# The attention block's output projection: seven products of quarters in two accumulation tiles, from the second image on

## The chip, the cores and the metric

The kernel runs on one core of a Trainium2 chip. A core has TensorE (PE, with its weight loads PEld), VectorE (DVE), ScalarE (ACT), GpSimd (POOL) and SyncE (SP), each with its own in-order queue, and 16 DMA engines that SP, ACT and POOL feed. The metric is the device time of one execution in microseconds, the median of several runs.

## The reference

Eight images of 512 channels by 32 x 32 positions pass two attention layers. Cut to what matters:

```python
# layer 0: eight heads, q, k and v quantized to 8 bits (fake_quant)
h = group_norm(xf, gn_w, gn_b)
q, k, v = split(einsum('oc,bct->bot', qkv_w, h) + qkv_b)
w = softmax(einsum('bct,bcs->bts', q * scale, k * scale))
a = einsum('bts,bcs->bct', w, v)
a = einsum('oc,bct->bot', proj_w, a) + proj_b        # the projection in question
x1 = xf + a
# layer 1: one head over all 512 channels
h = group_norm(x1, ...); q, k, v = h @ wq + bq, h @ wk + bk, h @ wv + bv
out = x1 + (softmax(q k^T / sqrt(512)) v) @ wp + bp
```

The projection is, per image, a 512 x 512 matrix times a 512 x 1024 matrix, all in float32; its bias is one number per channel.

## The kernel before, in words

Channels lie on the 128 partitions in four blocks (`cc`); the 1024 positions are cut into two halves (`hf`). A first phase computes q, k and v of all images and stores them in DRAM. The second phase, where the change lies, runs two things interleaved on every engine: the quantized attention of layer 0 (`attention`, L1018), which is one image ahead, and for the image whose attention is done the projection (`project`, L1296), the norm (`norm1`, L1344, through `norm_steps`, L228) and layer 1 (`layer1`, L1655).

Attention goes by units of 128 keys: a score product into the tile pair `st`, an exponential on ScalarE into `pt` (four buffers), a half-precision copy of it into `two` (by ScalarE, or by GpSimd for every fourth unit), the rest `two<-pt,two` by a VectorE subtraction, then the products `av` over the keys and the row sums `sm`. The sums of each pair of heads are inverted and `divide` (L1185, in `finish`, L1157) scales `ao`, the attention's output, two blocks of 512 columns per pair of heads.

Layer 1 computes its large products by a seven-product scheme for 2 x 2 quarters (`seven`, L1393, of Strassen and Winograd's kind): two PSUM tiles `x` and `y` of 128 x 512, each of them 2 x 256 columns of a quarter; a product is four matmuls of 256 columns for each 256 rows of contraction, and after it one of the outputs is taken out by VectorE or ScalarE while the other tile is filled. The sums and differences of quarters that it needs are VectorE work.

`project` is not in that form. For each half and each block of 128 output channels it adds up four matmuls of 512 columns in one PSUM tile. An eviction (`evict`, L1313) then adds the bias and the input x in place, `h<-pj,vec,h`, and SP stores the sum x1 to DRAM in `x1_d`, from where layer 1 loads it again for its output. A statistic per block (`stats`, L1319, BATCH_NORM_STATS2) is postponed as a chore, and in the second half an aggregate makes mean and variance `gmv` of it. `norm_steps` averages these over a group's channels by a tiny product with `gavg` (`gps_b`), computes the variance over the group, a second such product, and the scale.

From the second image on, `project` and the start of the norm stand inside the last output block of the image before (`o_run`, L1540, with `first` and `more`, L1764 to L1773): after its fourth product comes a piece of attention, the two halves of the projection with a piece of attention between them, another piece of attention, and then the block's three remaining products (`o`), with `gps_b` after the first of them. There the projection uses the two score tiles (`score_bank`, L315), and `load_wp` and `load_x2` (L1260, L1266) have the weights and the input loaded through ScalarE's queue ahead of the block. The last image's projection has no attention left beside it.

The order of each engine's instructions is written when the program is built. The class `InOrder` (L72) keeps a planned time for VectorE, ScalarE and TensorE; `do(cost, work)` puts work in at once with a planned cost, `later(name, cost, work, ...)` leaves it as a chore with a due time, `chore()` and `fill` put chores in where the plan has room, and `settle(name)` puts in all that are left of a name. `awaits` moves TensorE's planned time to that of a result. The planned times set only the order; on the chip each engine takes its instructions strictly in that order and waits where an operand is not ready.

Of the kernel before, what the change touches and what calls it, by code (L numbers as in the profile page):

```python
# [18 lines left out]
P = 128  # L19
# [39 lines left out]
def attn_pair_kernel(  # L59
# [166 lines left out]


    def norm_steps(  # L228
        src, dst, wcol, bank, nm, ccs=range(CC), fine=False, put=None, mv=None, apply=None
    ):  # L230

        n, c0 = len(ccs), ccs[0]
        put = put or (lambda hf, cost, work: work())
        if mv is None:
            st, mv = stat_tiles(n, nm)
            for i, cc in enumerate(ccs):
                for hf in range(NH):
                    dve.bn_stats(st[:, i, hf, :], src(cc, hf))  # L240
                aggregate(mv, st, i)
                if fine and i + 1 < n:
                    yield
        yield
        ps = bank(f"gps_{nm}")[:, 0:n]
        mm(ps, lhsT=gavg, rhs=mv[:, :, 0], start=True, stop=True)

        d = small.tile([P, n], F32, tag=f"gd{n}", name=f"gd_{nm}")
        mean = small.tile([P, n], F32, tag=f"gmean{n}", name=f"gmean_{nm}")

        def offsets():
            dve.tensor_sub(d, mv[:, :, 0], ps)
            dve.tensor_copy(mean, ps)
            dve.tensor_mul(d, d, d)
            dve.tensor_add(d, d, mv[:, :, 1])

        dve.do(0.6, offsets)
        yield
        ps2 = bank(f"gps2_{nm}")[:, 0:n]
        mm(ps2, lhsT=gavg, rhs=d, start=True, stop=True)  # L260
        rstd = small.tile([P, n], F32, tag=f"grstd{n}", name=f"grstd_{nm}")
        dve.do(0.15, lambda: dve.tensor_scalar(rstd, ps2, EPS, None, ALU.add))
        nc.gpsimd.tensor_tensor(rstd, rstd, mhalf[:, 0:n], ALU.pow)
        dve.do(
            0.15, lambda: dve.tensor_mul(rstd, rstd, vec[:, wcol + c0 : wcol + c0 + n]), dve.t + 1.4
        )
        if apply is not None:
            off = small.tile([P, n], F32, tag=f"goff{n}", name=f"goff_{nm}")
            dve.scalar_tensor_tensor(off, mean, -1.0, rstd, ALU.mult, ALU.mult)
            for i, cc in enumerate(ccs):  # L270
                apply(cc, rstd[:, i : i + 1], off[:, i : i + 1])
                yield
            return
        for hf in range(NH):
            for i, cc in enumerate(ccs):
                put(hf, 0.5, lambda i=i, cc=cc, hf=hf: dve.tensor_scalar(
                    dst(cc, hf), src(cc, hf), mean[:, i : i + 1], rstd[:, i : i + 1],
                    ALU.subtract, ALU.mult,
                ))
                if fine and i % 2 == 1:  # L280
                    yield
        if not fine:
            yield
# [23 lines left out]
    with ExitStack() as fast:  # L307
# [710 lines left out]
        def attention():  # L1018
# [138 lines left out]
            def finish(b, j, hf, u):  # L1157

                nm = f"{b}_{j}"
                if hf == 0:  # L1160
                    if b:
                        settle("ao")
                    ao[b, j] = aop.tile([P, NH, 512], F32, tag="ao", name=f"ao_{nm}")
                    if b == 0 and j % 2 == 1:
                        rss[b, j] = kept_u[:, 0:2].rearrange("p h k n -> p h (k n)")
                    else:
                        rss[b, j] = l1p.tile([P, NH, 512], F32, tag="rs", name=f"rs_{nm}")
                aot, rs = ao[b, j], rss[b, j]
                act.do(0.6, lambda: act.copy(aot[:, hf, :], avs.pop((b, j, hf))))
                act.do(0.6, lambda: act.copy(rs[:, hf, :], sms.pop((b, j, hf))))  # L1170
                if hf == 0:
                    return
                del rss[b, j]
                n = b * PAIRS + j

                apart = small.tile([P, 2, 16], F32, tag="apart", name=f"apart_{nm}")
                for w in range(2):
                    nc.sync.dma_start(
                        apart[:, w, :],
                        rs[2 * w * QUAD : 2 * (w + 1) * QUAD : QUAD].rearrange(  # L1180
                            "r h (p k) -> r h p k", k=16
                        ),
                    )

                def divide():  # L1185
                    dve.scalar_tensor_tensor(aot, aot, scl[:, 2:3], rs, ALU.mult, ALU.mult)

                def spread():
                    r = rcs[:, n * 16 : (n + 1) * 16]
                    dve.tensor_add(r, apart[:, 0, :], apart[:, 1, :])  # L1190
                    dve.reciprocal(r, r)
                    nc.sync.dma_start(rs_d[n].rearrange("r (p k) -> (r p) k", k=16), r)
                    for i, r in enumerate(HALF):
                        nc.sync.dma_start(
                            rs[r], rs_d[n][2 * i : 2 * i + 2, :].partition_broadcast(CH)
                        )
                    if InOrder.planned:
                        dve.later("ao", elements(1100), divide, dve.t + 7.0, 20.0)
                    else:
                        dealt.append((u + (20 if j < PAIRS - 1 else 13), "ao", divide))  # L1200

                if InOrder.planned:
                    dve.later("ao", 0.4, spread, pe.t + 5.0, 8.0)
                else:
                    dealt.append((u + (12 if j < PAIRS - 1 else 7), "ao", spread))
# [58 lines left out]
                dma(xts[b][:, :, bass.ts(hf, 512)], x_v[b, :, :, bass.ts(hf, 512)])  # L1264

        def load_wp(b, dma):  # L1266
            wps[b] = l2p.tile([P, CC, C], F32, tag="sums", name=f"wp0_{b}")
            dma(wps[b], w_sq[WP0])

        def load_first(u):  # L1270

# [21 lines left out]
            for t, src in zip(wm_tiles(b), wm_d):  # L1293
                act.dma_start(t, src)

        def project(b, bank=bank):  # L1296

            settle("ao")  # L1300
            st, mvs[b] = stat_tiles(CC, f"b{b}")
            wp0 = wps.pop(b)
            for hf in range(NH):
                for oc in range(CC):
# [6 lines left out]
                    xx = xts[b][:, oc, bass.ts(hf, 512)]  # L1311

                    def evict():  # L1313
                        dve.scalar_tensor_tensor(
                            xx, ps, vec[:, V_PB0 + oc : V_PB0 + oc + 1], xx, ALU.add, ALU.add
                        )
                        nc.sync.dma_start(x1_d[b][oc // 2][hf][:, oc % 2, :], xx)

                    def stats(oc=oc, hf=hf, xx=xx):  # L1319
# [24 lines left out]
        def norm1(b, bank=bank):  # L1344
# [14 lines left out]
                    put(hf, elements(512), work)  # L1359

            for n, _ in enumerate(norm_steps(
                at, at, V_GN1W, bank, f"b{b}", put=put, mv=mvs[b]
            )):
                if n == 2:
                    sums[b] = l2p.tile(
                        [P, 3, NH, CC // 2, 256], F32, tag="sums", name=f"sums2_{b}"
                    )
                    for hf in range(NH):
                        h11, h12, h21, h22 = quarters(b, hf)
                        t1, t2, t4 = (sums[b][:, i, hf] for i in range(3))  # L1370
                        for i, args in enumerate((
                            (t1, h12, h11), (t2, h22, t1), (h12, h22, h12), (t4, h21, t2)
                        )):
                            put_sum(hf, i, lambda args=args: tt(*args, ALU.subtract))
                yield
# [14 lines left out]
            dve.later("o", 0.25, spread, pe.t + 4.0, 5.0)  # L1390
            return rs

        def seven(nm, pairs, keep, whole, add, bank=bank):  # L1393

            nonlocal turn
            turn ^= 1  # L1400
            x, y = (bank(f"{nm}_{i}").rearrange("p (t n) -> p t n", t=2) for i in range(2))

            def product(n, ps, start):
                left, right = pairs[n]
                k = left.shape[1]
                for t in range(2):
                    for i in range(k):
                        mm(
                            ps[:, t, :], lhsT=left[:, i, bass.ts(t, P)], rhs=right[:, i, :],
                            start=start and t == 0 and i == 0, stop=(i == k - 1),  # L1410
                            skip_group_check=True,
                        )
# [4 lines left out]
                (5, x, False, whole, None),  # L1417
            )
            for i, (n, ps, start, out, m) in enumerate(work):
                awaits(free[(i + turn) % 2])  # L1420
                product(n, ps, start)
                free[(i + turn) % 2] = out(ps) if m is None else out(m, ps)
                yield i + 1

        free = [0.0, 0.0]
        turn = 0

        def slots(gq):
# [226 lines left out]
        def layer1(b, steps):  # L1655
# [46 lines left out]
            for hf in range(NH):  # L1702
# [59 lines left out]
                if b + 1 < B and last:  # L1762

                    def first():  # L1764
                        nonlocal ahead
                        yield -1
                        yield from project(b + 1, score_bank)
                        yield 2
                        ahead = norm1(b + 1, score_bank)
                        next(ahead)  # L1770

# [8 lines left out]
        def fold():  # L1780
# [36 lines left out]
            for i, (rows, lw, rw) in enumerate(((wa_rows, NQ1, NK1), (wm_rows, NV1, WP1))):  # L1817
# [29 lines left out]
                    load_first(24)  # L1847
                else:
                    dve.tensor_add(dst, tot, vec[:, V_BP : V_BP + CC])
            (m11, m12), (m21, m22), (v1, v2), (v3, v4) = ([t[:, i] for i in range(2)] for t in wm)  # L1850
            for args in (
                (v1, m11, m12, ALU.subtract), (v2, m22, v1, ALU.subtract),
# [452 lines left out]
```

## Time and profile before

| | |
|---|---|
| runs | 2558.69 us median of three (2558.62 to 2561.11) |
| profiled execution | 2559.32 us, its span 2557.2 us |
| granted TensorE clock | 0.999 |
| TensorE busy | 2515.9 us (98%) |
| VectorE busy | 1897.6 us (74%) |
| ScalarE busy | 1346.5 us (53%) |
| GpSimd busy | 186.0 us (7%) |
| DMA | 250.70 MB, mean 98 GB/s |
| pj matmuls (records of 512 columns) | 512, busy 224.1 us |
| evictions h<-pj,vec,h | 64 of 749 ns on average |

A row of groups gives the engine, the operation, what is written from what (buffer numbers left out), the shapes and the count; then the busy time, the mean of one record in nanoseconds, and the idle time of the engine just ahead of such an instruction with what ended it. A float32 matmul leaves two records. In the chain of waits each row is a start, a length and the engine that held up the end; in a timeline, a start, a length and, in brackets, how long the engine had been idle and for whom. Image numbers count from 0; image 2's projection runs from 1171.0 to 1203.5 us.

### The profile page before, as it was taken

To read this page: it belongs to the slowest core of one execution; us is meant where nothing else is said; L and a number is where in the kernel's file an instruction comes from. 1 tells how busy PE (TensorE), PEld (TensorE's weight loads), DVE (VectorE), ACT (ScalarE), POOL (GpSimd) and SP (SyncE) were. 2 spreads that over 40 slices of the span, in tenths; PEclk is the share of its full clock that TensorE was granted. 3 is DMA by queue.
4 is the path that set the end of the run, shared out by engine and by line. 5 is a ranking of instruction groups with operands and counts; after the bars stand their busy time and mean duration, and the time that the engine had idled before them with its cause. 6 is when DMAs were issued, how large, how long until landed. Compare 5 with 4: busy or idle time off the path is not lost.

```text
span 2557.2 us, 38727 instructions
## 1 busy us (share of the span) xinstructions
PE 2515.9 (98%) x15670; PEld 1746.2 (68%) x15670; DVE 1897.6 (74%) x2747; ACT 1346.5 (53%) x1685; POOL 186.0 (7%) x167
## 2 busy tenths in 40 slices
PE   8999999999999999999999999999999999999998
PEld 4788888873357756775777577667756775777787
DVE  7887776668887778777877787777778777885544
ACT  3332223319857655665666466656655665664121
POOL 0000000001100001000100100010101000100000
PEclk9999999999999999999999999999999999999999
DMA  4533333236622232223313222322232123212211
GB/s 168 177 142 125 131 124 122 109 131 162 162 88 63 79 116 85 58 74 122 98 57 100 92 79 78 110 92 63 79 112 88 55 71 128 96 42 80 87 38 39
DMA packets 160717, 250.70 MB, mean 98 GB/s; under 512 B 27152, under 2 KB 93712, under 8 KB 159120
## 3 DMA queue, kind: packets, MB, share of 16 engines
q1 hardware_dynamic: 125792, 182.81, 21.6%
q10 hardware_dynamic: 30560, 57.71, 6.5%
q0 software_dynamic: 4176, 7.60, 1.7%
q8 instruction: 125, 2.05, 0.3%
q14 instruction: 64, 0.52, 0.1%
HBM read 153.64 MB, written 86.28 MB: 94 GB/s over the span
## 4 chain that ended last, share of the span: by engine, by line
PE 85%; DVE 5%; ACT 2%; issue 1%; DMA 1%; POOL 0%; SPq 0%; ACTq 0%; DVEq 0%
PE s L209 15%; PE o L209 13%; PE qkps L209 12%; PE pj L209 8%; PE av L209 8%; PE v2ps L209 7%; PE vps L209 6%; PE g L209 6%; PE st L209 4%; PE sm L209 3%; DVE two L91 2%; ACT pt L91 1%; PE fold L209 1%; DVE h L91 1%; DVE acc L91 0%
## 5 line engine op out<-in xcount | busy, mean ns | idle before, releaser
L91 ACT ACTIVATE pt<-st,esc 128x1024 f32<-128x1024 f32 x467 | 496.4, 1114 | 332.1 <-PE st L209 317.6
L91 DVE TENSOR_TENSOR two<-pt,two 128x1024 f16<-128x1024 f32 x467 | 561.5, 1216 | 131.0 <-POOL two L1092 100.7
L91 ACT CAST two<-pt 128x1024 f16<-128x1024 f32 x346 | 350.8, 1055 | 6.9 <-ACT p L91 5.1
L1092 POOL CAST two<-pt 128x1024 f16<-128x1024 f32 x112 | 146.0, 1304 | 1409.4 <-PE sm L209 746.3
L209 PE MATMUL av<-two,v 128*32 128x512 f16 x3968 | 245.9, 381 | 2.5 <-DVE two L91 2.1
L209 PE MATMUL s<-g,h 128*128 128x256 f32 x1024 | 233.4, 380 | 0.0
L209 PE MATMUL pj<-ao,wp 128*128 128x512 f32 x512 | 224.1, 595 | 0.6 <-DVE h L91 0.6
L209 PEld LDWEIGHTS s<-g,h 128*128 128x128 f32 x1024 | 192.9, 190 | 31.0 <-issue 4.3
L91 ACT ACTIVATE u_ring<-qkps,qkbt 128x512 f32<-128x512 f32 x89 | 60.9, 685 | 243.8 <-PE qkps L209 219.3
L209 PEld LDWEIGHTS <-v 128*32 128x32 f16 x3968 | 91.8, 96 | 140.0 <-issue 66.7
L209 PEld LDWEIGHTS pj<-ao,wp 128*128 128x128 f32 x512 | 96.0, 190 | 122.5 <-issue 110.8
L209 PE MATMUL s<-g,sums 128*128 128x256 f32 x768 | 178.4, 381 | 0.2 <-DVE p L91 0.2
L209 PE MATMUL o<-p,v 128*128 128x256 f32 x768 | 175.2, 382 | 1.0 <-DVE p L91 1.0
L209 PE MATMUL st<-q,k 64*128 64x512 bf16 x1024 | 163.4, 382 | 11.9 <-ACT pt L91 7.5
L209 PEld LDWEIGHTS o<-p,v 128*128 128x128 f32 x768 | 144.3, 190 | 27.1 <-issue 5.7
L209 PEld LDWEIGHTS s<-g,sums 128*128 128x128 f32 x768 | 144.7, 190 | 24.2 <-issue 4.6
L209 PE MATMUL sm<-two,ones 128*32 128x512 f16 x1984 | 136.0, 379 | 0.0
L209 PEld LDWEIGHTS <-k 64*128 64x128 bf16 x1024 | 34.8, 94 | 143.8 <-issue 142.2
L209 PE MATMUL qkps<-half,w_high 128*128 128x512 f32 x480 | 132.4, 398 | 0.0
L209 PE MATMUL qkps<-half,w_mix 128*128 128x512 f32 x480 | 130.6, 394 | 1.0 <-DVE half L91 1.0
L209 PE MATMUL qkps<-half,w_low 128*128 128x512 f32 x480 | 130.5, 394 | 0.0
L209 PE MATMUL v2ps<-wm,h 128*128 128x256 f32 x512 | 119.9, 383 | 1.9 <-ACT g L91 1.3
(226 smaller groups left out, 3902.2 us busy)
## 6 DMA issues: line engine op xcount, KB each, us to landing
rs<-rs_d SPq DMA_DIRECT2D x76, 256.0 KB
x<-in_x_dram SPq DMA_DIRECT2D x32, 512.0 KB
q_d<-wa SPq DMA_DIRECT2D x32, 512.0 KB
k_d<-wa SPq DMA_DIRECT2D x32, 512.0 KB
v_d<-v_ring SPq DMA_DIRECT2D x32, 512.0 KB
raw<-q_d SPq DMA_DIRECT2D x32, 512.0 KB
raw<-k_d SPq DMA_DIRECT2D x32, 512.0 KB
x_d<-h SPq DMA_DIRECT2D x64, 256.0 KB
```

The lines of the kernel that those rows point to most:

```text
L91: ins = self.latest = op(*args, **kw).ins
L209: ins = nc.tensor.matmul(ps, lhsT=lhsT, rhs=rhs, **kw).ins
L1092: copy(two[:, 0], pt)
```

## The change

From the second image on, the projection is done by `seven` as well. The weights' four sums are made once, during image 0's projection (`combine_wp`), and written to DRAM in `wp_d`; later images load three of the quarters from the weights, and the sums from `wp_d`, the last of them into layer 1's tile `vt` by a load of its own in `project_seven`. The sums over the attention's output are made in place in `ao` and in a free part of `vt`. The three outputs of a product form that need two additions get both from VectorE into the tile of x itself: each of the seven products of a half is followed by one VectorE addition `h<-pj,h` of 2 x 256 columns, and the two PSUM tiles are the two score tiles, as before. The stores to `x1_d` go by quarters. The bias is no longer added at the eviction: it is added to the means ahead of `gps_b` and subtracted again from the group mean (`shift`), and added to `ob`, the bias of layer 1's output. Image 0 keeps the old form, without the bias.

```diff
@@ norm_steps
+        if shift is not None:
+            dve.do(0.15, lambda: dve.tensor_add(mv[:, :, 0], mv[:, :, 0], shift))
         ps = bank(f"gps_{nm}")[:, 0:n]
         mm(ps, lhsT=gavg, rhs=mv[:, :, 0], start=True, stop=True)
...
-            dve.tensor_copy(mean, ps)
+            if shift is None:
+                dve.tensor_copy(mean, ps)
+            else:
+                dve.tensor_sub(mean, ps, shift)
@@ finish, divide
                     dve.scalar_tensor_tensor(aot, aot, scl[:, 2:3], rs, ALU.mult, ALU.mult)
+                    if b and j == 1:
+                        first_sums(b)
@@ load_wp
-            wps[b] = l2p.tile([P, CC, C], F32, tag="sums", name=f"wp0_{b}")
-            dma(wps[b], w_sq[WP0])
+            wps[b] = w = l2p.tile([P, 6, CC // 2, C // 2], F32, tag="sums", name=f"wp0_{b}")
+            dma(w[:, 0:2].rearrange("p i k n -> p (i k) n"), w_sq[WP0][:, :, 0 : C // 2])
+            dma(w[:, 2], w_sq[WP0][:, CC // 2 :, C // 2 :])
+            dma(w[:, 3:6], wp_d[:, 0:3])
+        def combine_wp():
...
+            for args in (
+                (s1, a21, a22, ALU.add), (s2, s1, a11, ALU.subtract),
+                (s3, a11, a21, ALU.subtract), (s4, a12, s2, ALU.subtract),
+            ):
+                dve.later("wc", elements(512), lambda args=args: tt(*args), within=20.0)
+            dve.later("wc", 0.0, lambda: nc.sync.dma_start(wp_d, wc[:, 0:4]), within=20.0)
+        def first_sums(b):
+            for cc in range(CC // 2):
+                h = ao[b, cc]
+                dve.later("at", elements(512), lambda h=h: tt(
+                    h[:, :, 256:512], h[:, :, 256:512], h[:, :, 0:256], ALU.subtract
+                ), within=30.0)
+        def project_seven(b, room):
+            settle("at")
+            settle("ao")
+            st, mvs[b] = stat_tiles(CC, f"b{b}")
+            w = wps.pop(b)
+            a11, a12, a22, s2, s3, s1 = (w[:, i] for i in range(6))
+            t2 = room[:, 0 : NT // 2, 0:256].rearrange("p (k h) n -> p k h n", h=NH)
+            s4 = room[:, NT // 2 : NT // 2 + 2, 0:256]
+            act.dma_start(s4, wp_d[:, 3])
+            left, right = slice(0, 256), slice(256, 512)
+            def second(k):
+                tt(t2[:, k], ao[b, 2 + k][:, :, right], ao[b, k][:, :, right], ALU.subtract)
+            for k in range(2):
+                dve.do(elements(512), lambda k=k: second(k))
+            for hf in range(NH):
...
+                def into(q, row, col, full, hf=hf):
+                    def add(ps):
+                        there = dve.do(elements(512), lambda: tt(q, ps, q, ALU.add))
+                        if full is not None:
+                            nc.sync.dma_start(x1_d[b][row][hf][:, :, col * 256 : (col + 1) * 256], q)
+                        return there
+                    return add
...
+                for step in seven(
+                    f"pj_{b}_{hf}",
+                    ((a11, h11), (a12, h21), (s2, th), (s3, h11), (s1, t1), (s4, h22), (a22, h21)),
+                    lambda n, ps: keeps[n](ps), into(q12, 0, 1, 1), lambda n, ps: adds[n](ps),
+                    score_bank, True,
+                ):
+                    if step in (1, 2):
+                        for k in range(2):
+                            h = (h11, h21)[step - 1][k]
+                            args = (h, th[k], h) if step == 1 else (h, h, th[k])
+                            dve.do(elements(256), lambda args=args: tt(*args, ALU.subtract))
+                    for oc in {6: (2, 3), 7: (0, 1)}.get(step, ()):
+                        dve.later("pj", 0.62 + 0.2 * hf, lambda oc=oc, stats=stats: stats(oc), within=4.0)
+                    chore()
+                if hf + 1 < NH:
+                    yield -1
@@ project, image 0
-                        dve.scalar_tensor_tensor(
-                            xx, ps, vec[:, V_PB0 + oc : V_PB0 + oc + 1], xx, ALU.add, ALU.add
-                        )
+                        dve.tensor_tensor(xx, ps, xx, ALU.add)
@@ layer1, first
-                        yield from project(b + 1, score_bank)
+                        yield from project(b + 1, vt)
                         yield 2
+                        settle("pj")
                         ahead = norm1(b + 1, score_bank)
@@ fold
                     dve.tensor_add(dst, tot, vec[:, V_BP : V_BP + CC])
+                    dve.tensor_add(dst, dst, vec[:, V_PB0 : V_PB0 + CC])
```

`norm1` passes the projection's bias as `shift` in every image, and waits for the weight sums (`settle("wc")`) in image 0. `seven` takes a right operand as a list of blocks, and with its new argument `alone` it plans with two free tiles of its own.

## The prediction

> **What bounds the kernel now.** I read the page's parts 1 and 2 first, then the groups of part 5.
>
> ```profile
> PE 2515.9 (98%) x15670; PEld 1746.2 (68%) x15670; DVE 1897.6 (74%) x2747; ACT 1346.5 (53%) x1685; POOL 186.0 (7%) x167
> PEclk9999999999999999999999999999999999999999
> L209 PE MATMUL pj<-ao,wp 128*128 128x512 f32 x512 | 224.1, 595 | 0.6 <-DVE h L91 0.6
> ```
>
> TensorE is busy 98% at full clock, and the projection hardly waits (0.6 us). So TensorE time taken out counts, as long as nothing else becomes late. The price of both forms comes from the chain of waits over the whole span; its five longest pieces hold the last image's projection (no attention beside it), and a block in the seven-product form:
>
> ```profile
> 2362.57 27.47 PE pj L209 x64
> 2412.93 24.17 PE v2ps L209 x112
> ```
>
> Records: a float32 product leaves two. 64 records of 512 columns take 27.47 us (0.429 each), 112 of 256 columns 24.17 us (0.216 each).
>
> Next the chain in the window 1195 to 1225 us, around the end of image 2's projection, and the VectorE timeline over the same stretch:
>
> ```profile
> 1194.95 8.58 PE pj L209 x20
> 1203.54 0.98 PE av L209 x16
> ...
> 1207.45 3.65 PE o L209 x16
> 1211.10 0.12 PE gps_b L209 x2
> ```
> ```profile
> 1204.36 0.69 DVE L91 BATCH_NORM_STATS2 gst_b<-h 128x6 f32<-128x512 f32 x1
> 1205.09 0.21 DVE L91 BATCH_NORM_AGGREGATE gmv_b<-gst_b 128x2 f32<-128x12 f32 x1
> 1207.13 1.23 DVE L91 TENSOR_TENSOR two<-pt,two 128x1024 f16<-128x1024 f32 x1 [1.83 <-POOL two L1092]
> 1211.13 0.69 DVE L91 TENSOR_TENSOR kept_u<-o,kept_u 128x512 f32<-128x512 f32 x1 [2.78 <-PE o L209]
> ```
>
> After the projection TensorE needs 7.5 us to reach gps_b, the product that averages the means over groups. The means were ready at 1205.30, 5.6 us early. That slack is what the change spends. Last, the busy time by stretch (columns: length, PE, PEld, DVE, ACT, POOL):
>
> ```profile
> 1171.00:1185.00 14.00, 14.00 (x38) 6.05 (x35) 11.27 (x16) 4.04 (x6) 0.00 (x0) 1.00 0.55 170
> 1189.50:1203.50 14.00, 14.00 (x40) 6.03 (x40) 8.80 (x13) 3.46 (x4) 0.00 (x0) 1.00 0.24 87
> 1218.50:1240.00 21.50, 21.50 (x176) 14.70 (x172) 21.40 (x31) 15.25 (x21) 4.21 (x2) 1.00 0.34 117
> ```
>
> VectorE is free for 2.7 and 5.2 us in the two projection halves, and for 0.1 us in the stretch that starts 15 us later.
>
> **Part by part.** *The products.* Seven images go from 32 products of 512 columns to 56 of 256: 27.47 - 24.17 = 3.30 us each, 23.1 us in all. A rule speaks against this. The Trainium skill ("TensorE: Matmul & The Clock Gate", Back-to-back issue gap) says that in a stream of weight loads and matmuls the spacing depends on both, about 81 ns at 128 columns and 131 ns at 512, so narrower products are nearly as dear as wide ones. On a straight line between (my estimate from that page) 256 columns cost 98/131 = 0.75 of 512: the image would take 27.47 x 112/64 x 0.75 = 36 us, 8.6 us more than now and 60 us over seven. The rows say 0.216/0.429 = 0.50. They are of this kernel's float32 products, with one 190 ns weight load per record, so I take the row.
>
> *VectorE, per image.* Removed: eight evictions of 750 ns. Added: fourteen of 512 elements from PSUM (row p<-s,kept_u: 689 ns), four 512-element subtractions (687 ns) and eight of 256 elements, which no row shows in this form: 0.35 us (the 256-element tensor-scalar row, 347 ns) to 0.51 us (the x<-kept_u row); I take 0.42, as half of 687 plus the fixed part that the 4-element rows show (0.15). Sum: 14 x 0.69 + 2.75 + 3.4 - 6.0 = 9.8 us. Two of the 512-element ones come much earlier, at the second pair's division, in a stretch where VectorE is busy 16 to 17 of 20 us: cost nothing. The rest, 8.4 us, meets 7.9 us free in the two halves, which also get shorter by 3.3 us. So some of the present work must move, and the instruction order tells which: the four "two" subtractions (1.12 us from start to start in a row) that now stand between the evictions of the second half, and three of its four statistics (0.85 us each with the aggregate), all follow the last eviction; in the first half it is three "two" and three statistics.
>
> *Inside a half* I lay the in-order queues side by side: a product every 1.73 us, its eviction starting 0.29 us after it (as now), one 512-element operation every 0.61 us when queued. In the first half two second sums end before the first eviction; all evictions meet their product, and a tile is reused 0.7 us after it is free. Half one ends with 5.8 us of postponed vector work, done just before the first eviction of half two. No stall inside.
>
> *After the last product*, in VectorE order: wait 0.29, eviction 0.61, four "two" 4.48, three statistics 2.55, one "two" 1.12, the eviction kept_u<-o 0.61, the new addition of the bias to the means 0.20 with its hand-over: 9.86 us until gps_b may start. Now it starts after 7.46. The new wait is 2.4 us, with what is queued behind it on TensorE: two products of the output block and everything that follows. Its bounds: were no work postponed, the addition would still stand behind kept_u<-o, 0.29 + 0.61 + 0.20 = 1.1 us after that product; were everything as above and the "two" slowed by GpSimd's casts, perhaps 3. I take 2.4. Afterwards VectorE is free for some 2 us before the next eviction, so no debt reaches the full stretch.
>
> *ScalarE.* Three loads in place of one are issued at 1148 us, and a cast is queued behind an exponential. The chain there is vector work with no slack (kept_u, acc, p, then TensorE, from 1158.94 on), so up to 0.35 us; exponentials whose buffers wait for the postponed "two": up to 0.25. Below, both are nothing, since ScalarE has 1.55 us free at 1160.8. I take 0.1 in all.
>
> *DMA.* Weights grow from 1.0 to 1.75 MB per image plus 1 MB written once, 6.25 MB on 250.7. The load is issued at 1148 and wanted at 1171; queue 10 moved 57.71 MB in 6.5% of the span, about 350 GB/s while active, so 3.5 MB with the input need some 10 us. The last sum's 256 KB are issued at 1172 and wanted at 1181. The stores of x1 keep number and bytes in half as long rows; SP's fetch of the next v falls behind the first store, to 1175.5, and is wanted at 1195. Nothing, if the loads land within these margins; past them, microsecond for microsecond.
>
> *Image 0 and once.* Four sums for the combined weights: one stands ahead of the first eviction, which TensorE already awaits (0.65 us), so 0.6; three fall into an idle 2.4 us. The bias addition before gps_b, where nothing hides it: 0.2. Together 0.8 lost. *Image 7* has no attention beside it, so nothing is postponed but three statistics: 3.30 - 1.1 = 2.2 gained.
>
> **Sum.** Images 1 to 6: 3.30 - 2.4 - 0.1 = 0.8 each, 4.8; plus 2.2, minus 0.8: 6.2 us. The profiled execution took 2559.32 us (span 2557.2 and 2.1 around it), so 2553.1; it lay 0.6 above the median of the runs, 2558.69, so the median becomes 2552.5.
>
> **Rivals.** *Debt repaid early*: the postponed subtractions run in gaps that I miss, and only the 1.1 us behind kept_u<-o remain. For it: 15.7 us of VectorE idle between 1171 and 1218. Against: the queue is in order. 6 x 2.2 + 2.2 - 0.8 = 14.6, 2544. *All of it*: nothing waits, 23 us, 2535.6; against it stands the addition's place in the queue. *Gain eaten*: wait at gps_b 3 us and ScalarE's 0.6 in full: 6 x (-0.3) + 1.4, no change, 2556 to 2561. *Slower*: VectorE becomes the bound. Its work from the projection's start to gps_b, some 35 us, runs longer than reckoned, as TENSOR_SCALAR does beside GpSimd (0.74 us alone, one of 1.49 at 1168.56); the surplus delays gps_b one for one and, beyond 2 us, enters the full stretch. From 1.0 us per image the gain is gone, from 1.9 it is slower by 0.2%; at 2.5, 2561 to 2570. Against: two-source operations show few long records. *Narrow products dear*, as the rule says: about 2615. *Not doing what it says*: the order holds the seven products for images 1 to 7, so no.
>
> **How the numbers follow.** A measurement here tells some 0.2% (5.1 us) from no change: faster is below 2553.6. Likeliest case, 2549 to 2556, 0.56, of which 0.38 lies below; debt repaid 0.16; all 0.04; eaten 0.15; slower 0.08; rule 0.01. Faster 0.38 + 0.16 + 0.04 = 0.58, same 0.18 + 0.15 = 0.33, slower 0.09. The range reaches from 2544 to 2560; the likeliest case's own is 2549 to 2556.
>
> **What would show it.** Right: pj records 784 for images 1 to 7 at 0.216 us, each half's products within 12.3 us, gps_b waiting for DVE gmv_b by about 2.4 us in images 1 to 6 and 1.1 in image 7, kept_u<-o no longer idle before it. Wrong: waits among the products (evictions late), gps_b on time, PE waiting for a DMA of wp, or losses in the stretch after gps_b.

## The result, and the profile after

The changed kernel takes 2575.23 us (median of four runs, 2573.62 to 2578.86) against 2558.97 us for the kernel before (median of four by then): ratio 1.006, 95% interval 1.0048 to 1.0072. It is 16.3 us slower, where 6.2 us less had been forecast. The profiled execution of it took 2573.62 us, with a span of 2571.8 us, 14.6 more than before; the clock was 0.998.

The lines of the page and the group of the projection's products, after the change:

```profile
PE 2501.7 (97%) x16006; PEld 1811.0 (70%) x16006; DVE 1965.1 (76%) x2886; ACT 1348.8 (52%) x1685; POOL 188.7 (7%) x167
L209 PE MATMUL pj<-ao,wp 128*128 128x256 f32 (+1 forms) x624 | 155.1, 404 | 1.0 <-DVE h L91 1.0
```

The last row holds the products that read ao and wp; with those that read the sums, images 1 to 7 have 784 records, as forecast. TensorE is busy 14 us less: the products give the 23 us (12.30 us a half in the chain below, for 13.95), while the av and st records, which now wait, show 6.5 more. The first half of image 2 in the chain of before:

```profile
1171.09 13.95 PE pj L209 x32
```

VectorE is busy 67 us more, about as reckoned. The span less TensorE's busy time rose from 41.3 to 70.1 us, so the question is where TensorE waits. I cut both spans at two kinds of record on TensorE's timeline, the first pj of an image and its gps_b, and compare the pieces (image 0's row starts at the span's start):

| stretch (us) | before | after | difference | forecast |
|---|---|---|---|---|
| start to gps_b of image 0 | 727.9 | 729.0 | +1.2 | +0.8 |
| six times gps_b to the next image's first pj | 1204.8 | 1216.5 | +11.7 | +0.6 |
| six times first pj to gps_b, images 1 to 6 | 239.5 | 240.1 | +0.6 | -5.4 |
| gps_b of image 6 to first pj of image 7 | 190.2 | 190.3 | +0.1 | 0 |
| image 7, first pj to gps_b | 30.9 | 30.9 | 0.0 | -2.2 |
| gps_b of image 7 to the end | 163.9 | 164.9 | +1.0 | 0 |

Most of the loss, 1.9 us in each of six images, lies where the prediction looked for 0.1: ahead of the projection. Laid side by side, the two TensorE timelines run in step from gps_b for 182 us and part at one block of attention. TensorE's waits there follow from ScalarE's timeline. Before:

```profile
1148.06 0.60 ACT L91 ACTIVATE p<-s 128x512 f32<-128x512 f32 x1 [0.37 <-PE s L209]
1148.06 0.35 ACTq L91 DMA_DIRECT2D wp<-in_w_sq_dram  x1
1148.45 1.00 ACTq L91 DMA_DIRECT2D h<-in_x_dram  x2
1149.50 1.05 ACT L91 CAST two<-pt 128x1024 f16<-128x1024 f32 x1 [0.85 <-ACT p L91]
1151.51 0.58 ACT L91 COPY kept_u<-o 128x512 f32<-128x512 f32 x1 [0.96 <-PE o L209]
```

and after, at the same place:

```profile
1151.26 0.60 ACT L91 ACTIVATE p<-s 128x512 f32<-128x512 f32 x1 [0.37 <-PE s L209]
1151.26 1.59 ACTq L91 DMA_DIRECT2D wp<-in_w_sq_dram  x2
1152.90 0.48 ACTq L91 DMA_DIRECT2D wp<-wp_d  x1
1153.42 1.00 ACTq L91 DMA_DIRECT2D h<-in_x_dram  x2
1154.71 0.58 ACT L91 COPY kept_u<-o 128x512 f32<-128x512 f32 x1 [2.86 <-DMA wp<-in_w_sq_dram]
1155.19 1.12 ACT L91 ACTIVATE pt<-st,esc 128x1024 f32<-128x1024 f32 x1
1156.20 1.04 ACT L91 CAST two<-pt 128x1024 f16<-128x1024 f32 x1
```

ACTq rows are transfers that ScalarE issues; p<-s runs beside the first of them, and no other ScalarE work starts until the last is issued. From the start of p<-s to the cast it took 1.44 us and now takes 4.94, in all six images. The three weight loads are issued in 2.04 us here (0.56, 1.00 and 0.48; some 1.7 in the other images) where one took 0.35, but that is not what makes the cast late. The eviction kept_u<-o starts 3.45 us after p<-s in both kernels, just as its products o end on TensorE, and the last issue has ended before that, 2.86 to 3.16 us after p<-s. (The bracket of the eviction names a load; the signal of the products comes 0.02 us ahead of the start, as in the kernel before.) What changed is the order: the planner, which counts half a microsecond for each issue, now puts the cast behind that eviction and an exponential, where before it ran while ScalarE waited for the products.

The cast feeds a two subtraction on VectorE and that the products av. On TensorE, after:

```profile
1151.06 3.62 PE L209 MATMUL o<-p,v 128*128 128x256 f32 x16
...
1157.30 0.40 PE L209 MATMUL av<-two,v 128*32 128x512 f16 x4 [0.68 <-ACT two L91]
1158.56 0.40 PE L209 MATMUL av<-two,v 128*32 128x512 f16 x4 [0.86 <-DVE two L91]
```

In TensorE's list of waits (us in total, times, longest), over 700 to 2400 us of the changed kernel, the first rows are:

```profile
PE gps_b L209 <- DVE gmv_b L91: 13.2, 7, 2.2
PE av L209 <- DVE two L91: 7.2, 12, 0.9
PE st L209 <- ACT pt L91: 4.4, 14, 0.4
PE av L209 <- ACT two L91: 4.1, 6, 0.7
```

and of the kernel before:

```profile
PE st L209 <- DVE h L91: 3.1, 6, 0.5
PE st L209 <- ACT pt L91: 2.8, 7, 0.4
```

with no row of av, nor of gps_b. The wait for ACT two is new (0.68 six times); of the 7.2 us for DVE two, 0.86 six times lie at the same place, and 0.34 six times behind the projection.

The gps_b row is the wait that was forecast. The chain around the end of image 2's projection shows how it comes about:

```profile
1193.40 12.30 PE pj L209 x56
...
1205.72 0.69 DVE h L91
1206.42 5.38 DVE two L91 x4
1211.79 0.62 DVE gst_b L91
...
1214.24 1.09 DVE two L91
1215.33 0.60 DVE kept_u L91
1215.93 0.08 DVE gmv_b L91
1216.01 0.14 issue
1216.15 0.36 PE gps_b L209 x2
```

From the last product of the projection to gps_b the chain is all VectorE's, 10.45 us in place of 7.4: last eviction, four postponed subtractions, statistics, one more subtraction, kept_u, bias. On TensorE these 3.1 us are the 2.16 at gps_b, 0.34 at the av before it, and av and st records that are longer by the rest. The busy times of the two halves and of the stretch that starts 15 us later (columns as before):

```profile
1176.10:1190.10 14.00, 13.54 (x76) 11.06 (x76) 11.14 (x19) 5.16 (x7) 0.00 (x0) 1.00 0.49 144
1191.90:1205.90 14.00, 14.00 (x90) 11.28 (x92) 12.50 (x22) 4.72 (x5) 0.48 (x1) 1.00 0.25 78
1223.70:1245.20 21.50, 21.50 (x177) 14.78 (x176) 21.41 (x30) 15.15 (x21) 3.92 (x2) 1.00 0.33 111
```

VectorE still idles 2.9 us in the first half while its subtractions wait for the half's end: the gaps between two evictions are 1.12 us (a product every 1.73, an eviction 0.61 from start to start), a two takes 1.13, and the planner, which reckons 1.19, put only the quantization steps of 0.75 us in.

### The profile page after: what moved, and what is told of

Read it like the earlier page. It is cut to its first block, busy times and chain, and to the rows that moved or that the text cites. A ratio compares the mean times of both kernels' runs of the same rounds, so it can differ in the third digit from the quotient of the medians.

```text
span 2571.8 us, 39622 instructions
## 1 busy us (share of the span) xinstructions
PE 2501.7 (97%) x16006; PEld 1811.0 (70%) x16006; DVE 1965.1 (76%) x2886; ACT 1348.8 (52%) x1685; POOL 188.7 (7%) x167
## 3 DMA queue, kind: packets, MB, share of 16 engines
q8 instruction: 127, 2.08, 0.4%
## 4 chain that ended last, share of the span: by engine, by line
PE 77%; DVE 11%; ACT 3%; issue 3%; DMA 2%; POOL 1%; SPq 0%; DVEq 0%; ACTq 0%; POOLq 0%
PE s L209 15%; PE o L209 12%; PE qkps L209 12%; PE v2ps L209 7%; PE pj L209 7%; PE vps L209 6%; PE av L209 6%; PE g L209 5%; DVE two L91 5%; PE st L209 3%; PE sm L209 3%; DVE h L91 2%; ACT pt L91 1%; DVE sums L91 1%; DVE kept_u L91 1%
## 5 line engine op out<-in xcount | busy, mean ns | idle before, releaser
L91 DVE TENSOR_TENSOR two<-pt,two 128x1024 f16<-128x1024 f32 x467 | 569.9, 1240 | 123.2 <-POOL two L1098 69.2
L209 PEld LDWEIGHTS s<-g,h 128*128 128x128 f32 x1024 | 193.0, 190 | 30.9 <-issue 4.3
L209 PE MATMUL pj<-ao,wp 128*128 128x256 f32 (+1 forms) x624 | 155.1, 404 | 1.0 <-DVE h L91 1.0
L209 PEld LDWEIGHTS pj<-ao,wp 128*128 128x128 f32 x624 | 117.2, 190 | 35.7 <-issue 19.1
```

Source lines behind the costliest of these rows:

```text
L91: ins = self.latest = op(*args, **kw).ins
L209: ins = nc.tensor.matmul(ps, lhsT=lhsT, rhs=rhs, **kw).ins
```

## The experiments

**ScalarE's queue against the transfers.** First, the same three loads, issued by SyncE:

```diff
-                    load_wp(b + 1, act.dma_start)
+                    load_wp(b + 1, nc.sync.dma_start)
```

> Theory S (ScalarE's queue): the 1.9 us that each of six images loses ahead of its projection come from ScalarE, which issues three weight loads instead of one and has a cast queued behind them. With the three loads issued by SyncE, ScalarE's order is again that of the kernel before, so 6 x 1.9 = 11.4 us come back: about 2564 us, and gps_b to the next projection lasts about 200.5 us again. Rival D (the transfers): more bytes and shorter rows are in the way of other transfers, whoever issues them: no change, 2573 to 2577 us, and the same 202.4 us.

Measured: 2566.75 us against 2559.72 of the kernel before, measured beside it (ratio 1.0028, 1.0016 to 1.0039). The stretch from gps_b to the next projection is 200.4 us in the images 1 and 4, as in the kernel before, with every byte as in the changed kernel. In the images 2, 3 and 5 it is 202.1, and that is another thing: it is lost directly behind gps_b. TensorE's timeline there, in this kernel:

```profile
1455.36 0.36 PE L209 MATMUL gps_b<-gmv_b,gavg 128*128 128x4 f32 x2 [2.16 <-DVE gmv_b L91]
1455.58 5.39 PE L209 MATMUL o<-g,v 128*128 128x256 f32 x16
```

and its clock, the third column from the right, in windows of the same stretch:

```profile
1455.00:1457.00 2.00, 1.64 (x9) 1.51 (x10) 1.15 (x9) 1.02 (x2) 0.00 (x0) 0.99 0.07 7
1457.00:1459.00 2.00, 2.00 (x6) 1.61 (x5) 0.56 (x2) 0.00 (x0) 0.00 (x0) 0.50 0.06 8
1459.00:1461.00 2.00, 2.00 (x9) 1.58 (x7) 0.00 (x0) 0.00 (x0) 0.00 (x0) 0.66 0.32 121
```

The 16 products take 5.39 us in place of 3.70: 1.69 us lost at half clock, after a wait of 2.16 us. So the 1.9 us come from ScalarE, as theory S says, and a second cost was found that neither theory had.

**One load.** `wp_d` holds all seven quarters in the tile's order, and image 0 writes the three plain ones there too:

```diff
-            dma(w[:, 0:2].rearrange("p i k n -> p (i k) n"), w_sq[WP0][:, :, 0 : C // 2])
-            dma(w[:, 2], w_sq[WP0][:, CC // 2 :, C // 2 :])
-            dma(w[:, 3:6], wp_d[:, 0:3])
+            dma(w, wp_d[:, 0:6])
...
```

> All seven quarters are kept in DRAM in the order of the tile, so ScalarE issues one load of 1.5 MB in place of three. Theory S: one issue of about 0.5 us instead of 2.0 us, and the cast stands ahead of the eviction again; 10 to 11.4 us come back, 2564 to 2566 us. Rival D: the bytes are the same, so 2573 to 2577 us if the volume counts; if the short rows of 1 KB are what costs, it gains here but not where SyncE issues the same three loads.

Measured: 2567.85 us (1.0031, 1.0019 to 1.0042). The issue took 0.34 us, and the cast stood ahead of the eviction again, 1.4 to 2.6 us after p<-s. The expected 2564 to 2566 were missed by some 2 to 4 us; the clock fell behind gps_b in five of six images, which alone is 8.5 us.

**The cast's place alone.** The planner's time for ScalarE is put back by 1.0 behind the loads, so that the cast goes ahead of the eviction; nothing else moves:

```diff
                     load_wp(b + 1, act.dma_start)
+                    act.t -= 1.0
```

> The three loads stay with ScalarE, and only the cast behind them goes back ahead of the eviction kept_u<-o and one exponential. The cast was 3.5 us late against its place in the kernel before: 1.7 by longer issuing, 1.8 by its place, and 1.6 of it was covered. If both add up, either alone is nearly covered: the loss falls from 1.9 to about 0.2 us per image, 2565 us. If the issuing alone is the cause and the place doesn't matter: 2574 us. If moving the cast only shifts the wait to the eviction and the exponential: 2570 us or more.

Measured: 2568.83 us (1.0037, 1.0024 to 1.0049). Issuing still took 2.8 to 3.3 us, so the cast came 2.9 to 3.4 us after p<-s, yet the stretch to the next projection was 200.5 and 200.4 us in images 1 and 2; the clock fell in the other four. So the loss follows the place, and the issuing is covered. The sum in the expectation (1.7 us by issuing, 1.8 by place) does not hold: with the eviction fixed at 3.45 us by TensorE, the place makes the whole 3.5 us, however short the issuing. The short issuing with the late place was not run.

**The loads alone, in the kernel before.**

```diff
-            dma(wps[b], w_sq[WP0])
+            w, src = wps[b], w_sq[WP0]
+            dma(w[:, :, 0 : C // 2], src[:, :, 0 : C // 2])
+            dma(w[:, CC // 2 :, C // 2 :], src[:, CC // 2 :, C // 2 :])
+            dma(w[:, 0 : CC // 2, C // 2 :], src[:, 0 : CC // 2, C // 2 :])
```

> The kernel before, with nothing of the change but its one weight load cut into three of the same bytes (four, two and two rows of 256 columns per partition). By theory S it loses the same 1.9 us in six images, 11 us: 2568 to 2571 us, without a single product, sum or byte changed. By rival D, or if VectorE's added work is the cause of that loss: no change, 2559 us.

Measured: 2571.46 us (1.0044, 1.003 to 1.0058), 11.7 us more. Its list of waits opens with the av rows of the changed kernel, less the 0.34 us waits behind the projection:

```profile
PE av L209 <- DVE two L91: 5.2, 6, 0.9
PE av L209 <- ACT two L91: 4.1, 6, 0.7
```

The cast stands 4.94 us after p<-s again, and the six stretches take 1217.7 us for 1204.8, so the cut load alone, by way of the planner's order, costs what the change lost there (11.7). Rival D is out for these stretches: the same bytes in the same short rows cost nothing when SyncE issued them.

**The bias alone, in the kernel before.** The eviction becomes a plain addition, and the means get the bias ahead of gps_b, as in the change:

```diff
+        if shift is not None:
+            dve.do(0.15, lambda: dve.tensor_add(mv[:, :, 0], mv[:, :, 0], shift))
         ps = bank(f"gps_{nm}")[:, 0:n]
...
```

> The kernel before with the bias part of the change alone: the eviction no longer adds the bias, and the means get it just ahead of gps_b, behind the eviction kept_u<-o. Theory Q (place in VectorE's queue): gps_b, which waited for nothing, now waits for an eviction that cannot start before its product is done, about 1.0 us in each of seven images (image 7 of the changed kernel shows 1.02) and 0.24 in image 0: 7.3 us more, about 2567 us. Rival: four elements per partition cost 0.15 us and are hidden: 2559 to 2560 us.

Measured: 2567.82 us against 2560.4 (1.003, 1.0018 to 1.0042): 7.4 us more. Its waits:

```profile
PE gps_b L209 <- DVE gmv_b L91: 5.9, 7, 0.9
```

These are 0.95 in images 1 to 6 and 0.24 in image 0; image 7, behind the window, shows 0.92. Four numbers per partition cost 0.95 us an image, because they stand behind an eviction whose product has only just ended. The clock did not fall behind any of these waits. (In the profiled execution it fell ahead of image 0's projection, some 1.5 us.)

**The subtractions between the evictions.** One number of the planner:

```diff
-                    if begin + cost > limit + 0.15:
+                    if begin + cost > limit + InOrder.slack:   # 0.6 in project_seven, else 0.15
...
```

> The changed kernel with one number of the planner altered during the projection: work may be put between two evictions if it delays the next by up to 0.6 us of the plan, in place of 0.15. The subtractions called two then stand between the evictions instead of behind the last one. Theory P (placing): VectorE has the time, the work was only queued in the wrong place, so the wait at gps_b falls from 2.16 to about 1.0 us (what the addition of the bias costs) and the 0.9 us of small waits around it go: 2.0 us in six images, 2563 us. Rival F (VectorE is full there): the evictions become late and TensorE waits among the products, or the debt comes back in the stretch behind: 2573 to 2577 us.

Measured: 2559.82 us (0.9999, 0.9991 to 1.0007), 15.4 less than the changed kernel. First pj to gps_b went from 40.0 to 37.7 us, and gps_b waits 0.94, what the bias costs. The gaps of 1.12 us took the subtractions in, and no product waited for an eviction in images 1 to 6. Theory P holds, by more than expected (2.3 us an image for 2.0). The 202.3 us to the next projection stay, since the loads are as they were.

The same with the one load:

> The last kernel with the one load of 1.5 MB in place of three. Theory P with S: against the one load alone (2567.8) the same 2.0 us in six images, and without waits of 2.2 us the clock has no reason to fall behind gps_b, which cost 1.7 us in five images there: 2567.8 - 12 - 8.5 = 2547 us. Rival F: 2566 us. Had the clock fallen for another reason than the wait: 2556 us.

Measured: 2545.36 us (0.9947, 0.9934 to 0.9961): 15 us faster than the kernel before. The gap to the next projection is back at 200.4 us in four of five images (201.6 in image 4, see below), and the clock fell behind no gps_b.

**All three mends.** Loads and subtractions as in the last kernel; the addition moves ahead of the generator's first `yield`, right behind the last statistic:

```diff
+        if shift is not None:
+            dve.do(0.15, lambda: dve.tensor_add(mv[:, :, 0], mv[:, :, 0], shift), dve.t)
         yield
-        if shift is not None:
-            dve.do(0.15, lambda: dve.tensor_add(mv[:, :, 0], mv[:, :, 0], shift))
```

> The last kernel with the addition of the bias put right behind the last statistics, ahead of the eviction kept_u<-o. If theory Q holds, gps_b waits for nothing any more: 1.0 us less in seven images, 2540 us, nearly the 23 us that the products save. Rival: VectorE reaches the statistics no earlier than the eviction: 2547 us as the last.

Measured: 2547.89 us (0.9951, 0.9937 to 0.9964), no gain on the last: the expectation failed, though first pj to gps_b did fall by 1.1 us to 36.6. The list of waits shows where it went:

```profile
PE g L210 <- ACT vsum L92: 6.6, 6, 2.2
```

ScalarE's eviction to vsum is late, since an exponential ahead of it waits for a two on VectorE, and VectorE had stood at the transfer apart<-rs of the row sums. In image 1 VectorE stood 2.08 us, the exponential waited 2.46 and TensorE 0.55; in images 4 and 6 it was 3.51, 4.14 and 2.21. There the clock fell too, and the stretch lost 3 to 4 us against the last kernel. In the kernel before, VectorE stands at this transfer for 0.9 to 1.3 us, and TensorE does not wait for vsum. In image 4 of the last kernel it stood 2.65 us, and TensorE waited 0.55.

> The kernel with all three mends, with one due time changed: the division's row-sum step (rcs), which stands at the head of VectorE's queue behind gps_b and waits 2.1 us there for a transfer, is planned 7 us instead of 5 after its sums, so two ready operations go ahead of it. Theory H (head of the queue): the 1.1 us won at gps_b were lost 15 us later because the exponentials' buffers wait for VectorE, which idles at this transfer; with it moved, the waits of TensorE for vsum (6.6 us) and the two falls of the clock behind them (4 and 2 us) go: 2547.9 - 11 = 2537 us. Rival F (VectorE has too much work there, idle or not): 2546 to 2549 us.

The edit is one number, `pe.t + 7.0` for `pe.t + 5.0` at the chore `spread` in `finish`. Measured: 2542.12 us (0.9929, 0.9916 to 0.9943), the fastest, 18.6 us under the kernel before. The waits for vsum are gone, as theory H says; but about half of what was expected came back ahead of the next projection (the first row is 1.0 in the kernel before, the second is not there):

```profile
PE o L210 <- DVE p L92: 3.7, 6, 0.6
...
PE sm_l L210 <- DVE acc L92: 1.2, 6, 0.2
```

**The clock.** To tell the wait from other causes, the kernel with one load and the subtractions in their gaps got a longer wait and nothing else on the path:

```diff
+        if shift is not None and not nm.endswith("b0"):
+            for hf in range(NH):
+                dve.bn_stats(small.tile([P, 6], F32, tag="idle", name=f"idle_{nm}_{hf}"), src(0, hf))
```

> The kernel with one load and the new places of the subtractions (2545.4), with two superfluous statistics of 0.64 us put on VectorE just ahead of the addition to the means in images 1 to 7; the results are not used. Theory C (the clock follows the wait): gps_b waits about 2.2 us instead of 0.95, 9 us in all, and as in 13 of 18 such waits seen so far the products behind it run at half clock for 3.5 us, 1.7 us each in about 5 of 7 images: 2562 us, and 5.4 us for the 16 products behind gps_b where it happens. Rival: the clock fell for another reason (more work per us, other transfers): 2554 to 2555 us, all blocks 3.7 us.

Measured: 2556.77 us (0.9986, 0.9979 to 0.9993), between the two. In the profiled execution the clock fell behind two of the seven waits, as here in image 5, and not behind the other five:

```profile
1926.42 0.36 PE L210 MATMUL gps_b<-gmv_b,gavg 128*128 128x4 f32 x2 [2.13 <-ACT two L92]
1926.64 5.39 PE L210 MATMUL o<-g,v 128*128 128x256 f32 x16
```

(The bracket names ScalarE; gps_b reads gmv_b, behind the two statistics.) The longer wait itself cost 1.2 us an image. So the wait brings falls back, as theory C says, but five in seven was too many: the 13 of 18 behind it had left out the six waits of the changed kernel, none of which had a fall.

## Why the prediction was wrong

The step that failed first is ScalarE's: "Three loads in place of one are issued at 1148 us, and a cast is queued behind an exponential. The chain there is vector work with no slack (kept_u, acc, p, then TensorE, from 1158.94 on), so up to 0.35 us". With 0.25 for the exponentials it was taken as 0.1 in all. The prediction saw the edit and the new place of the cast, but priced them by one issue, and along the wrong path. The path is cast, two subtraction, av; on it the cast is 3.5 us later than before, since the eviction ahead of it waits for TensorE; 1.6 of that were covered. This cost 1.9 us in each of six images. It is shown by the change's own profile, by its going when SyncE issues the loads or when the cast alone is put back, and by its coming in the kernel before when only its load is cut. 11.1 us of the miss of 20.8 in the span are this.

The second is the wait at gps_b. Its mechanism was right: 2.16 us measured in six images, and 1.02 in image 7 for 1.1. But the 2.4 us were the growth of the whole tail, and that is 3.1 us. Three of the four postponed subtractions took 1.13 or 1.14 us as reckoned; the last took 1.98 to the next start, beside a cast of GpSimd that took 1.90 for 1.04 before. "Half one ends with 5.8 us of postponed vector work, done just before the first eviction of half two" missed 0.3 us between the halves, where one subtraction took 1.98 us too, beside a cast of 1.38. Over the changed kernel 13 of 476 subtractions took about 2.06 us, each beside such a cast, and the others at most 1.23; but 24 of these ran beside a cast too, for over 0.3 us, so what the two do to each other stays open. Together it is 1.0 us an image, 6 us, so that the stretch which should gain 0.9 us loses 0.1. This is the bound of 3 us that the prediction gave for slowed subtractions, and its rival "gain eaten", in that stretch.

Image 7 should have gained 2.2 us and gained nothing. "No stall inside" failed there: TensorE waited 0.58 and 1.01 us among the products, and the first half took 14.37 us for 12.25 in the second. The 2 KB transfer of the row sums, which stands at the head of VectorE's queue ahead of the first eviction, took 6.34 us where it took 2.9 before, and the next one, which the second wait follows, is issued only after it:

```profile
2379.34 0.18 DVE L91 RECIPROCAL rcs<-spread_l 128x4 f32<-128x4 f32 x1 [3.93 <-DMA spread_l<-rs]
```

The loads are issued 14 us before this projection (25 in image 2), and the DMA engines were full (share 1.04 from 2373 to 2376 us). In the variants with the same tail the image's time follows that transfer: 28.8 us with 4.1 or 4.5 (one load), and with three loads from ScalarE 29.6 with 5.1, 30.4 with 5.9, 30.9 with 6.3 (where SyncE issued them it was 29.1, and the trace does not show when the transfer ended). So "nothing, if the loads land within these margins" held for the weights, for which TensorE never waited, and failed for a small transfer behind them. The one load has the same bytes as the three, so the number of bytes alone does not set the delay; what does was not tried by itself.

Image 0 and the start lost 1.2 us for 0.8. A fall of the clock after a wait of 1.59 us, ahead of the projection, took about 1.5 and the eviction's earlier end gave 0.8 back; 0.5 was there before and stays unexplained. Of the 1.0 us behind image 7, 0.9 come after the last vector operation; runs of the other variants differ by as much, and it was not followed up.

Right were the price of the products (12.30 us a half, so the row and not the rule), VectorE's sum, the two early sums and, in images 1 to 6, the DMA volume costing nothing, and that no debt of VectorE reached the full stretch. The last held with the wait at gps_b in place: once it was taken away, waits on VectorE turned up there (vsum, then p and acc). The rival "slower" came nearest in time, but its cause, a full VectorE, is not what the runs show; of the signs of being wrong, losses in the stretch after gps_b came, at its end and by way of ScalarE, and in image 7 waits among the products.

## What to carry to other kernels

Where the order on each engine is fixed when the program is built, an edit can cost by moving something else in that order. Here two more issues of half a microsecond in the plan put a ready cast behind an eviction that waits for TensorE, 3.5 us late. So compare the order on every engine before and after, and price a moved instruction by what it now stands behind, not by the instruction that was added. A tiny operation costs what stands ahead of it in an in-order queue, here 0.95 us for 0.15. And a saving on the bound engine was kept here only where the work it postpones was put back between other work: with one load, one planner number, the bias ahead and one due time the same seven products are 0.7% faster instead of 0.6% slower.

## What was not expected of the hardware

A wait of TensorE of 2.1 to 2.2 us at gps_b was followed by 3.41 us at half clock in 15 of 31 cases over the profiles of five kernels (0 of 6 in the changed kernel, 5 of 6 with one load), at 1.7 us each; a wait of 1.5 to 1.6 us, ahead of image 0's projection, in 4 of 12 kernels; a wait of 0.92 to 1.02 us at gps_b in none of 25. The Trainium skill ("TensorE: Matmul & The Clock Gate", Why this matters for your kernels) advises against gaps of more than about 3 us; here half of that sufficed at times, and the measurement decides.

Why some images and not others can be read from when the falls begin. With one load the clock fell at 971.54, 1213.89 and 1456.24 us, 71 times 3.413 us apart, and in every profile with more than one its falls begin a whole number of 3.413 us apart. So the clock behaves as if it were set once in each cell of a fixed grid. Laid on that grid, each of the 15 waits at gps_b with a fall had at least 1.78 us inside one cell; of the 16 without, 15 had at most 1.75, and one 1.96. An image of the changed kernel takes 242.3 us, close to 71 cells (242.35), so its six waits lie at nearly the same place of the grid (1.36 to 1.65 us in one cell) and are one draw of luck rather than six. The skill's section "What's actually happening" says that the window is free-running, which agrees with such a grid. The waits ahead of image 0's projection do not sort this way (falls with 0.87 to 1.46 us in one cell, none with up to 1.54), so this is a pattern of the long waits and not the whole rule.
